# Layer 3's depthwise taps in 64x64 tiles, by a table of slots

## The chip, the cores and the metric

The kernel runs on one core of a Trainium2 chip. The metric is device time in microseconds (us), the median of the timed runs.

## What is computed

Four layers work on x of 4 samples, 256 channels, 48x48 positions, in float32. Layer 0 is an attention over eight heads with normalised queries and keys, layer 1 a gate from depthwise convolutions, layer 2 a second attention; each adds its result to x. Layer 3 is what the change touches:

```
def _L3_conv_ref(x, attn_w1, attn_w2, refine_w, refine_b):
    p = jnp.mean(x, axis=(2, 3))
    h = leaky_relu(p @ attn_w1.T, SLOPE)
    a = sigmoid(h @ attn_w2.T)
    y = x * a[:, :, None, None]
    y = conv_general_dilated(y, refine_w, (1, 1), 'SAME', feature_group_count=C)   # 3x3 depthwise
    y = y + refine_b[None, :, None, None]
    mu = mean(y, (2, 3)); var = mean(square(y - mu), (2, 3))
    return leaky_relu((y - mu) * rsqrt(var + EPS), SLOPE)
...
x = x + _L3_conv_ref(_gn(x), ...)
```

`_gn` normalises groups of eight channels of a sample.

## The kernel before, in words

Channels lie on the 128 partitions, in two halves k; a sample is thus two tiles of 128 x 2304, and layer 3 has eight tiles, cut into six slices of 384 columns (8 rows of 48) each. The engines' instruction streams are written out by hand: each engine runs its own in order.

**Before layer 3.** The last unit of layer 2's attention ends with `total_here`, `fold` and `divide`; `w_stats` (L1062) then takes the last statistics of layer 2's output, from which L1335 to L1348 make the scale sc2 and shift bi2. Layer 1 has taps on TensorE too (L893): diagonal weights in 64x64 tiles, taps of a row half written to both column halves of a bank. Attention (L270, L290) uses 64x64 tiles as well, and alternates between the row halves.

**`Pre`** makes a sample ready. A step is one third of a half sample: four 64x64 matmuls (L1377) give layer 2's output in two banks, ACT normalises it into tmp (L1384), DVE or POOL adds it to X (L1408), DVE takes two `bn_stats` (L1413). `first` (L1388) does the whole of the first sample ahead of the loop, `add` (L1396) the later ones inside it. `chain` (L1417) then turns the statistics into the group norm and the channel gate a, by small matmuls and small DVE instructions; `rsqrt` (L168) is a power on POOL. It ends with ACT filling two padded images `pad` of 50 x 50 (L1476), scaled by rsa and shifted by nba.

**`Conv`** works on one tile. `products` (L1495) puts four of the nine taps on TensorE, each a 128x128 diagonal times a shifted window of the pad, for one slice. `taps` (L1508) does the other five for a pair of slices g, on DVE, in PSUM. `evict` (L1519) moves the pair to z on ACT, with bias and sum; `square` (L1531) sums the squares about a centre; `scales` and `shift` (L1538, L1551) make the instance norm, with rsqrt on POOL (in_ri) and a small product on DVE (in_mr, L1553); `scale` (L1557, ACT) and `leak` (L1561, DVE) finish z; `gain` (L1565, POOL, DVE at the end) adds it to X; `store` writes out.

**The order** is the loop at L1608: over the eight tiles, and in each over six slices, a list of ifs says what goes out in which slice, with the tile before (`prev`) finished during this one and `older` stored. The scores' and values' PSUM tiles (sc two pairs of banks, av one) carry the products; pj has two banks.

**The verdict** (L1580 to L1588) checks that the softmax sums are in bounds, once, before layer 3; it decides at the end whether a general path runs, which does not happen here.

Of the kernel before, what the change touches and what calls it, by code (L numbers as in the profile page):

```python
# [74 lines left out]
def usual_path(  # L75
# [8 lines left out]
    ps_sc = ctx.enter_context(tc.tile_pool(name="ps_sc", bufs=2, space=bass.MemoryType.PSUM))  # L84
    ps_av = ctx.enter_context(tc.tile_pool(name="ps_av", bufs=1, space=bass.MemoryType.PSUM))
    ps_pj = ctx.enter_context(tc.tile_pool(name="ps_pj", bufs=2, space=bass.MemoryType.PSUM))

# [987 lines left out]
    PE_TAPS = (0, 1, 2, 3)  # L1075
    DVE_TAPS = (4, 5, 6, 7, 8)
    diag = {}

    def diagonals():

        for k in range(NK):
            xs = xsp.tile([P, NK, SL + 1], F32, tag="xs", name="diag")
            xs = xs.rearrange("p k s -> p (k s)")[:, : len(PE_TAPS) * P]
            diag[k] = xs.rearrange("p (t j) -> p t j", j=P)
            for n, t in enumerate(PE_TAPS):
                nc.gpsimd.tensor_scalar(
                    diag[k][:, n, :], ident, rfw[:, k, t : t + 1], None, ALU.mult
                )
                yield 1
# [260 lines left out]

    W2 = HW + 2
# [5 lines left out]
    GW = 2 * SL  # L1357

# [5 lines left out]
    class Pre:  # L1364


        def __init__(self, n):
            self.n, self.b = n, SEQ[n]
            self.st = small.tile([P, NK, NSL, 6], F32, tag="gn_st", name="gn_st")
            self.steps = [(k, c) for k in range(NK) for c in range(L2C)]  # L1370
# [17 lines left out]
        def first(self, i, eng):  # L1388

            ps = two_banks(i)  # L1390
            self.product(i, [ps[:, h, :SL] for h in range(2)])
            tmp = wk.tile([P, 2, SL], F32, tag="tmp", name="tmp")
            self.normed(i, tmp, ps[:, :, :SL])
            self.gain(i, tmp, eng)

        def add(self, i):  # L1396
            halves = [pj_tile()[:, :SL] for _ in range(2)]
            self.product(i, halves)
            tmp = wk.tile([P, 2, SL], F32, tag="tmp", name="tmp")
            for h in range(2):  # L1400
                self.normed(i, tmp[:, h, :], halves[h])
            self.gain(i, tmp, nc.gpsimd)
# [7 lines left out]
        def stats(self, i):  # L1410
            k, c = self.steps[i]
            for s in (c, c + L2C):
                nc.vector.bn_stats(  # L1413
                    self.st[:, k, s, :], X[self.b][:, k, s * SL : (s + 1) * SL]
                )

        def chain(self):  # L1417

            mv = small.tile([P, NK, 2], F32, tag="gn_mv", name="gn_mv")
            for k in range(NK):  # L1420
                nc.vector.bn_aggr(mv[:, k, :], self.st[:, k].rearrange("p s f -> p (s f)"))
            yield
            ps = pj_tile()
            nc.tensor.matmul(ps[:, 0:NK], lhsT=gmat, rhs=mv[:, :, 0], start=True, stop=True)
            yield
            gm = small.tile([P, NK], F32, tag="gn_gm", name="gn_gm")
            nc.vector.tensor_copy(gm, ps[:, 0:NK])
            dev = small.tile([P, NK], F32, tag="gn_dev", name="gn_dev")
            nc.vector.tensor_sub(dev, mv[:, :, 0], gm)
            sq = small.tile([P, NK], F32, tag="gn_sq", name="gn_sq")  # L1430
            nc.vector.tensor_mul(sq, dev, dev)
            nc.vector.tensor_add(sq, sq, mv[:, :, 1])
            yield
            ps = pj_tile()
            nc.tensor.matmul(ps[:, 0:NK], lhsT=gmat, rhs=sq, start=True, stop=True)
            yield
            gv = small.tile([P, NK], F32, tag="gn_gv", name="gn_gv")
            nc.vector.tensor_scalar(gv, ps[:, 0:NK], GN_EPS, None, ALU.add)
            rs = small.tile([P, NK], F32, tag="gn_rs", name="gn_rs", bufs=6)
            rsqrt(rs, gv)  # L1440
            yield
            yield

            pm = small.tile([P, NK], F32, tag="pm", name="pm")
            nc.vector.tensor_mul(pm, dev, rs)
            nb = small.tile([P, NK], F32, tag="gn_nb", name="gn_nb", bufs=6)
            nc.vector.scalar_tensor_tensor(nb, gm, -1.0, rs, ALU.mult, ALU.mult)
            yield
            ps = pj_tile()
            for k in range(NK):  # L1450
                nc.tensor.matmul(
                    ps[0:D, 0:1], lhsT=w1[:, k, :], rhs=pm[:, k : k + 1],
                    start=k == 0, stop=k == NK - 1,
                )
            raw = small.tile([D, 1], F32, tag="hraw", name="hraw")
            nc.vector.tensor_copy(raw, ps[0:D, 0:1])
            hl = small.tile([D, 1], F32, tag="hl", name="hl")
            nc.vector.scalar_tensor_tensor(hl, raw, SLOPE, raw, ALU.mult, ALU.max)
            yield
            ps = pj_tile()  # L1460
            for k in range(NK):
                nc.tensor.matmul(
                    ps[:, k : k + 1], lhsT=w2[:, k * P : (k + 1) * P], rhs=hl,
                    start=True, stop=True,
                )

            ga = small.tile([P, NK], F32, tag="ga", name="ga")
            nc.scalar.activation(ga, ps[:, 0:NK], AF.Exp, scale=-1.0)
            nc.vector.tensor_scalar(ga, ga, 1.0, None, ALU.add)
            nc.vector.reciprocal(ga, ga)  # L1470
            rsa = small.tile([P, NK], F32, tag="rsa", name="rsa")
            nc.vector.tensor_mul(rsa, rs, ga)
            nba = small.tile([P, NK], F32, tag="nba", name="nba")
            nc.vector.tensor_mul(nba, nb, ga)
            for k in range(NK):
                nc.scalar.activation(  # L1476
                    pads[(self.n * NK + k) % NPAD][:, 1 : 1 + HW, 1 : 1 + HW],
                    X[self.b][:, k, :].rearrange("p (r c) -> p r c", c=HW), AF.Identity,
                    bias=nba[:, k : k + 1], scale=rsa[:, k : k + 1],
                )  # L1480
                yield

    class Conv:


        def __init__(self, i):
# [3 lines left out]
            self.z = big.tile([P, N], F32, tag="qk"[i // 2 % 2], name="z")  # L1490

            self.st = small.tile([P, 2, NG3], F32, tag="in_st", name="in_st", bufs=3)
            self.ps = {}

        def products(self, s):  # L1495
            g = s // 2
            if s % 2 == 0:
                self.ps[g] = two_banks(self.i * NG3 + g)
            for n, t in enumerate(PE_TAPS):
                dr, dc = divmod(t, 3)  # L1500
                nc.tensor.matmul(  # L1501
                    self.ps[g][:, s % 2, :SL].rearrange("p (r c) -> p r c", c=HW),
                    lhsT=diag[self.k][:, n, :],
                    rhs=self.pad[:, s * RS + dr : (s + 1) * RS + dr, dc : dc + HW],
                    start=n == 0, stop=n == len(PE_TAPS) - 1,
                )

        def taps(self, g):  # L1508
            z = self.ps[g][:, :, :SL].rearrange("p h (r c) -> p h r c", c=HW)
            for t in DVE_TAPS:  # L1510
                dr, dc = divmod(t, 3)
                r0 = 2 * g * RS + dr
                src = self.pad[:, r0 : r0 + 2 * RS, dc : dc + HW]
                nc.vector.scalar_tensor_tensor(  # L1514
                    z, src.rearrange("p (h r) c -> p h r c", h=2),
                    rfw[:, self.k, t : t + 1], z, ALU.mult, ALU.add,
                )

        def evict(self, g):  # L1519
            nc.scalar.activation(  # L1520
                self.z[:, g * GW : (g + 1) * GW].rearrange("p (h s) -> p h s", h=2),
                self.ps[g][:, :, :SL], AF.Identity, bias=vec[:, V_RB, self.k : self.k + 1],
                accum_out=self.st[:, 0, g : g + 1],
# [54 lines left out]


    ok = lp.tile([P, 2, LW], F32, name="ok")  # L1580
    nc.vector.tensor_scalar(ok[:, 0, :], lsum, SUM_HI, None, ALU.is_le)
    nc.vector.tensor_scalar(ok[:, 1, :], lmin, SUM_LO, None, ALU.is_ge)
    okm = lp.tile([P, 1], F32, name="okm")
    nc.vector.tensor_reduce(okm, ok, AX.XY, ALU.min)
    ps = pj_tile()
    nc.tensor.matmul(ps[0:1, 0:1], lhsT=okm, rhs=ones[:, 0:1], start=True, stop=True)
    sound = lp.tile([1, 1], mybir.dt.int32, name="sound")
    nc.vector.tensor_scalar(sound, ps[0:1, 0:1], P - 0.5, None, ALU.is_ge)  # L1588

    pres = {0: Pre(0), 1: Pre(1)}  # L1590
# [933 lines left out]
```

## Time and profile before

| what | us |
|---|---|
| runs, median of 3 | 3661.74 (3661.73 to 3662.2) |
| profiled execution, its own time | 3660.4 |
| its span | 3658.6 |
| first matmul of layer 3's convolution (L1501) | starts at 3431.1 |
| last DVE tap (L1514) ends | 3642.2 |
| PE busy, whole span | 3499.3 (96%) |
| DVE busy, whole span | 2617.0 (72%) |
| mean granted TensorE clock | 0.982 of full speed |

The span is the time from the first to the last instruction of one profiled execution; PE is TensorE, DVE VectorE, ACT ScalarE, POOL GpSimd, SP the engine that issues most transfers. On the page, the rows of digits cut the span in 40 slices and give the busy share in tenths. A group's row has the line, the engine, the operation, output <- inputs, shape and count; after the bar its busy time and mean duration in ns; after the next bar the engine's idle time just before it and what ended it.

### The profile page before, as it was taken

Reading aid. Unit: us, or ns where it says so; the run is one execution under the profiler, and the core shown is the slowest. Engines: PE = TensorE matmul, PEld = TensorE weight load, DVE = VectorE, ACT = ScalarE, POOL = GpSimd, SP = SyncE. Lnnn points to the kernel's source line nnn. Section 1 sums busy time; section 2 is a strip of 40 time slices with the busy share of each in tenths; the row PEclk is TensorE's granted clock in tenths of the full one; section 3 lists DMA queues with packets and bytes.
Section 4 is the critical chain, followed back from the end, with each engine's and each line's share of the span. In section 5 each row is a group of like instructions: output and inputs, shape, how many; then the busy total and the mean of one; then the engine's idle time right before and its main releaser. Section 6 shows DMA issues by size and latency. Waiting matters only on the chain. (4 is left out here: it accounts for less than half of the span.)

```text
span 3658.6 us, 86475 instructions
## 1 busy us (share of the span) xinstructions
PE 3499.3 (96%) x36338; PEld 1778.0 (49%) x36338; DVE 2617.0 (72%) x3227; ACT 2381.9 (65%) x3814; POOL 1389.8 (38%) x881
## 2 busy tenths in 40 slices
PE   8999999999999999999999999999999999999685
PEld 4555555454444445544444444444444445654343
DVE  3555555476989786869896868688967687576687
ACT  4665666666875886668758866687588555555353
POOL 2333333333333333333333333333333366664232
PEclk9999999999999999999999999999999999999797
DMA  2111111111111111311111111111111100000001
GB/s 91 47 25 21 27 22 25 21 25 21 26 21 25 21 26 21 77 21 25 21 25 21 25 21 26 21 26 21 30 13 30 13 6 6 6 8 4 26 39 66
DMA packets 113534, 95.52 MB, mean 26 GB/s; under 512 B 56192, under 2 KB 110064, under 8 KB 111600
## 3 DMA queue, kind: packets, MB, share of 16 engines
q1 hardware_dynamic: 110240, 87.73, 13.1%
q8 instruction: 286, 4.69, 0.5%
q10 hardware_dynamic: 2896, 2.18, 0.2%
q14 instruction: 112, 0.92, 0.1%
HBM read 56.97 MB, written 11.80 MB: 19 GB/s over the span
## 5 line engine op out<-in xcount | busy, mean ns | idle before, releaser
L276 ACT ACTIVATE pt<-sc 128x768 f32<-128x768 f32 x1944 | 1475.3, 811 | 768.2 <-PE sc L270 759.9
L301 POOL TENSOR_TENSOR half<-pt 128x768 f32<-128x768 f32 x477 | 948.7, 1990 | 1607.9 <-ACT pt L276 1512.2
L270 PE MATMUL sc<-q,k 64*64 64x384 f32 x13824 | 1273.3, 483 | 5.1 <-ACT pt L276 5.1
L290 PE MATMUL av<-pt,v 64*64 64x384 f32 x13824 | 1276.4, 484 | 0.0
L316 DVE TENSOR_TENSOR acc<-acc,pt 128x768 f32<-128x768 f32 x792 | 962.1, 1215 | 81.0 <-DVE acc L316 1.9
L270 PEld LDWEIGHTS sc<-q,k 64*64 64x64 f32 x13824 | 521.0, 133 | 607.9 <-issue 537.3
L290 PEld LDWEIGHTS av<-pt,v 64*64 64x64 f32 x13824 | 518.6, 133 | 592.2 <-issue 559.5
L316 DVE TENSOR_TENSOR acc<-acc,half 128x768 f32<-128x768 f32 x459 | 475.1, 1035 | 306.3 <-POOL half L301 305.1
L653 DVE SCALAR_TENSOR_TENSOR x<-pj,bo,x 128x384 f32<-128x384 f32 x192 | 118.3, 616 | 435.3 <-PE pj L648 434.8
L826 ACT ACTIVATE prod<-pd,wt 128x256 f32<-128x256 f32 x486 | 335.9, 761 | 0.2
L566 PE MATMUL pj<-xs,w 128*128 128x384 f32 (+1 forms) x720 | 275.4, 505 | 0.9 <-POOL xs L510 0.9
L371 POOL TENSOR_TENSOR o<-o,rinv 128x384 f32<-128x384 f32 x95 | 119.0, 1253 | 358.0 <-DMA rinv<-rinv 336.1
L566 PEld LDWEIGHTS pj<-xs,w 128*128 128x128 f32 x720 | 124.1, 189 | 128.9 <-issue 35.9
L290 PE MATMUL av<-pt,qv 64*64 64x384 f32 x1728 | 178.0, 503 | 0.0
L648 PE MATMUL pj<-o,wo 128*128 128x384 f32 x384 | 162.0, 506 | 14.8 <-DVE x L653 7.2
L270 PE MATMUL sc<-qv,kd 64*64 64x384 f32 x1728 | 172.3, 491 | 2.4 <-ACT pt L276 2.4
L849 DVE TENSOR_REDUCE prod<-prod 128x256 f32<-128x1280 f32 x114 | 168.4, 1477 | 4.1 <-ACT prod L826 4.1
L310 DVE TENSOR_TENSOR acc<-pt 128x768 f32<-128x768 f32 x99 | 150.6, 1521 | 10.7 <-ACT pt L276 10.7
L597 PEld LDWEIGHTS pj<-w,xs 128*128 128x128 f32 x1080 | 134.5, 191 | 24.1
L597 PE MATMUL pj<-w,xs 128*128 128x128 f32 x1080 | 134.9, 275 | 0.0
L367 POOL TENSOR_TENSOR o<-raw 128x384 f32<-128x384 f32 x95 | 117.6, 1238 | 0.0
L582 ACT ACTIVATE k<-pj,bias 128x384 f32<-128x384 f32 x90 | 52.3, 581 | 95.3 <-PE pj L566 94.8
(234 smaller groups left out, 2672.0 us busy)
## 6 DMA issues: line engine op xcount, KB each, us to landing
xs<-in_x_dram SPq DMA_DIRECT2D x90, 384.0 KB
rinv<-rinv SPq DMA_DIRECT2D x208, 94.5 KB
out_dram<-x SPq DMA_DIRECT2D x6, 1152.0 KB
l<-row SPq DMA_DIRECT2D x416, 1.5 KB
w<-in_wqkv_dram SPq DMA_DIRECT2D x32, 192.0 KB
x<-in_x_dram SPq DMA_DIRECT2D x4, 1152.0 KB
x<-in_x_dram SPq DMA_DIRECT2D x9, 384.0 KB
rinv<-ls SPq DMA_DIRECT2D x208, 1.5 KB
```

Of the source, the lines that this page charges most:

```text
L270: nc.tensor.matmul(ps[c * D : (c + 1) * D, h, :SL], lhsT=u["of"]["k"][r, j0 : j0 + D], rhs=u["of"]["q"][r, u["qc"]], start=True, stop=True,)
L276: nc.scalar.activation(pt, ps[:, :, :SL], AF.Exp, scale=u["scale"])
L290: nc.tensor.matmul(u["av"][h * D : (h + 1) * D, half, :SL], lhsT=value(u, j, h)[r], rhs=pt[r, h, :], start=j == 0, stop=j == JB - 1,)
L301: nc.gpsimd.tensor_add(half, pts[0], pts[1])
L310: nc.vector.tensor_add(u["acc"], ready[0], ready[1])
L316: nc.vector.tensor_add(u["acc"], u["acc"], term)
L371: eng.tensor_mul(o, o, u["rinv"])
L566: nc.tensor.matmul(ps[:, :n], lhsT=at["w"][:, k, t, :], rhs=xs[s][:, k, :n], start=k == 0, stop=k == NK - 1,)
L597: nc.tensor.matmul(ps[:, i * P : (i + 1) * P], lhsT=xs[s][:, k, i * P : (i + 1) * P], rhs=at["w"][:, k, 2, :], start=k == 0, stop=k == NK - 1,
L648: nc.tensor.matmul(ps[:, :SL], lhsT=wo[:, p, k * P : (k + 1) * P], rhs=o["o"], start=True, stop=True,)
L826: nc.scalar.activation(bufs[n % 3][:, :, min(n, 1) + i].rearrange("p (r c) -> p r c", c=AS), pd[:, PAD + dr : PAD + dr + AS, PAD + dc : PA ...
L849: nc.vector.tensor_reduce(to, bufs[n % 3][:, :, : min(n, 1) + len(taps)], AX.X, ALU.add)
```

## The change

Eight of the nine taps go to TensorE, in 64x64 tiles; DVE keeps the middle one (4). A slice uses two banks, each a PSUM tile of its own in a pool of six. Bank h holds the products of channel half h: even taps in its own half of the partitions, odd taps in the other. DVE adds the middle tap to the first sum and writes z; ACT copies the second sum with the bias to `part`, across to the channels' own partitions; a `join` of the pair adds both and sums them.

```
-    PE_TAPS = (0, 1, 2, 3)
-    DVE_TAPS = (4, 5, 6, 7, 8)
+    PE_TAPS, DVE_TAP = (0, 1, 2, 3, 5, 6, 7, 8), 4
...
-                    diag[k][:, n, :], ident, rfw[:, k, t : t + 1], None, ALU.mult
+                    diag[k][:, n, :], ident2, rfw[:, k, t : t + 1], None, ALU.mult
...
+    rb_x = lp.tile([P, NK], F32, name="rb_x")
+    for to, fr in zip(HALVES, HALVES[::-1]):
+        nc.sync.dma_start(rb_x[to, :], vecs[fr, V_RB, :])
...
         def products(self, s):
...
+            self.ps[s] = [ps_one.tile([P, 512], F32, tag="one", name="one") for _ in HALVES]
+            now["ps"] = self.ps[s][0]
+            last = len(PE_TAPS) // 2 - 1
+            for n in range(last + 1):
+                for h, r in enumerate(HALVES):
+                    for e in range(2):
+                        nc.tensor.matmul(
+                            self.ps[s][h][HALVES[h ^ e], :SL].rearrange(
+                                "p (r c) -> p r c", c=HW
+                            ),
+                            lhsT=diag[self.k][r, 2 * n + e, :],
+                            rhs=self.window(r, s, PE_TAPS[2 * n + e]),
+                            start=n == 0, stop=n == last,
+                        )
...
         def evict(self, s):
...
+            for h, r in enumerate(HALVES):
                 nc.vector.scalar_tensor_tensor(
+                    z[r], self.window(r, s, DVE_TAP), rfw[r, self.k, DVE_TAP : DVE_TAP + 1],
+                    self.ps[s][h][r, :SL].rearrange("p (r c) -> p r c", c=HW),
+                    ALU.mult, ALU.add,
+                )
+                nc.scalar.activation(
+                    self.part[g][HALVES[1 - h], s % 2, :], self.ps[s][1 - h][r, :SL],
+                    AF.Identity, bias=rb_x[r, self.k : self.k + 1],
+                )
+
+        def join(self, g):
+            z = self.z[:, g * GW : (g + 1) * GW]
+            nc.vector.tensor_tensor_reduce(
+                z, z, self.part[g].rearrange("p h s -> p (h s)"), 1.0, 0.0, ALU.add, ALU.add,
+                self.st[:, 0, g : g + 1],
+            )
```

The loop is replaced by a table: each job is put at a slot t (one slot per slice, 48 and a few more) with a rank, and the slots are written out one after the other.

```
+    FRONT, PRODUCT, CONV, EVICT, SMALL, NEXT, THEN, LAST, OUT = range(9)
...
+    def put_step(t, n, i, gap=1):
+        at(t, PRODUCT, lambda: pres[n].multiply(i))
+        at(t, NEXT, lambda: pres[n].evict(i))
+        at(t, OUT, lambda: pres[n].gain(i, pres[n].tmp, nc.gpsimd))
+        at(t + gap, LAST, lambda: pres[n].stats(i))
...
+    for n in range(1, B):
+        t = (n - 1) * SAMPLE
+        if n > 1:
+            for i in range(STEPS):
+                put_step(max(3, t - 10 + 2 * i), n, i)
+        put_chain(t + 4, pres[n].chain())
+        for k in range(NK):
+            for i in range(NG3):
+                at(t + 10 + k * NSL + 2 * i, LAST, lambda n=n, k=k, i=i: pres[n].pad(k, i))
...
+    def put_tile(t, cv, final):
         for s in range(NSL):
+            at(t + s, CONV, lambda s=s: cv.products(s))
+            at(t + s + 1, EVICT, lambda s=s: cv.evict(s))
+        for g in range(NG3):
+            at(t + 2 * g + 3, NEXT, lambda g=g: cv.join(g))
+            at(t + 2 * g + 4, THEN, lambda g=g: cv.square(g))
+        at(t + 3, THEN, cv.centre)
+        dt = 9 if final else 10
+        at(t + dt, THEN, cv.scales)
+        at(t + dt + 1, FRONT, cv.shift)
+        for g, cols in enumerate(THIRDS):
+            t0, dt = (t + 10 + g, 1) if final else (t + 11 + 2 * g, 2)
+            at(t0, THEN, lambda cols=cols: cv.scale(cols))
+            at(t0 + 1, NEXT, lambda cols=cols: cv.leak(cols))
+            eng = nc.vector if final else nc.gpsimd
+            at(t0 + 1 + dt, OUT, lambda cols=cols: cv.gain(cols, eng))
+            at(t0 + 1 + dt, OUT, lambda cols=cols: cv.store(cols))
```

Further: pad, scale, leak, gain and store now go in thirds of a tile. The chain's small products land in columns 384 and up of a slice's first bank, and its parts have a slot each. Three steps of the second sample (`filled`) are multiplied during the first sample's chain, in the sc and av banks, before these are given back for the pool of six. The verdict moves into slots 6 and 7 of the table. In the built program's order the first three products of layer 3 stand ahead of the last `w_stats` on TensorE. Lines of the changed kernel that the prediction names: products L1541, DVE's tap L1559, ACT's copy L1564, join L1571, square L1583, shift L1603, scale L1609, leak L1613, gain L1617.

## The prediction

> **What bounds the kernel now.** I read the page first, then busy time by stretch for the last 370 us, then the groups and the timeline of that stretch.
>
> ```profile
> PE   8999999999999999999999999999999999999685
> DVE  3555555476989786869896868688967687576687
> PEclk9999999999999999999999999999999999999797
> ```
>
> TensorE (PE) bounds the first 3395 us; there the two programs differ only in the small GpSimd (POOL) instructions that build the diagonals. Layer 3 is the last two or three slices, so at most some 7% of the time can move.
>
> ```profile
> 3436.00:3458.00 22.00, 17.91 (x76) 8.17 (x72) 15.08 (x21) 7.93 (x15) 7.39 (x5) 1.00 0.00 1
> 3458.00:3480.00 22.00, 19.84 (x61) 10.22 (x62) 15.26 (x34) 9.55 (x16) 6.65 (x5) 0.77 0.00 1
> 3600.00:3620.00 20.00, 17.34 (x53) 9.35 (x51) 19.08 (x21) 6.20 (x10) 5.87 (x4) 1.00 0.14 59
> ```
>
> Columns: stretch, length, busy time of PE, weight loads, DVE, ACT, POOL, then the clock. In layer 3 DVE is the fullest (19.08 of 20 late on); ACT has less than half. The clock holds 1.00 with PE 81% busy and falls after a PE gap of 3.4 us that ends at 3458.4. The groups say what fills DVE:
>
> ```profile
> L1514 DVE SCALAR_TENSOR_TENSOR sc<-pad,rfw,sc 128x768 f32<-128x768 f32 x80 | 81.7, 1021 | 2.3
> L1514 DVE SCALAR_TENSOR_TENSOR av<-pad,rfw,av 128x768 f32<-128x768 f32 x40 | 40.6, 1016 | 1.1
> L1520 ACT ACTIVATE z<-sc,vec 128x768 f32<-128x768 f32 x16 | 14.4, 900 | 57.2 <-DVE sc L1514 50.9 <-PEq L2450 6.3
> ```
>
> Five taps make 5.25 us for two slices, 126 us in all, and ACT's eviction waits 51 us for them. From nba (3428.6) to the last tap (3642.2) are 213.6 us for 24 pairs of slices, 8.9 a pair; then 16.4 us to the end.
>
> **TensorE, part by part.** Before, a slice is 4 matmuls of 128x128x384, 8 instructions, 2.6 us. After, it is 16 of 64x64, 32 instructions. Attention runs 16 such instructions in 1.29 us, so 2.58. [...] Attention alternates row groups; the new loop issues two tiles of one group in a row. If they took turns, two tiles would run instead of four: 5.2 us a slice. But layer 1's taps (L893) have exactly this order:
>
> ```profile
> 3046.18 2.87 PE L893 MATMUL pj<-pd,diag 64*64 64x256 f32 x48
> 3048.82 1.52 PE L290 MATMUL av<-pt,qv 64*64 64x384 f32 x16
> ```
>
> 48 in 2.64 us are 55 ns each; times 384/256 and 32, 2.64 us. I take that: eight taps cost what four did. With a step (0.65) and small products a pair is 5.5 to 6.1 us on PE, not the bound.
>
> **DVE and ACT, per pair of slices.** Removed: 5.25 of taps on DVE, 1.1 of eviction on ACT. Added: DVE, four taps of 64x384 from PSUM. No row has 64 partitions; 128x384 from PSUM (L653) is 0.617, and ACT's 64x384 (0.576) is near its 128x384 (0.581), so 0.617. ACT, four `part` copies at 0.576 (L1014, which also crosses partitions). And the join, a sum with a running total, no row: SBUF add 0.96 (DVE L1567) plus a read of the total near ACT's 0.19, 1.12 together. [...] Leak (L1563), that kind with two fp32 SBUF sources but without a total, does 128x768 in 0.95[...]; I take 1.12 and keep 1.92 for the range; below nothing is excluded, since it is new work. Thirds in place of whole tiles: pad 0.9 for 768 columns (2.31 whole), scale 0.95, leak 0.96.
>
> **A wait that comes in.** In the changed program's order of instructions DVE's second tap of a slice waits for ACT's first copy, and ACT's second copy for DVE's first tap, since they read the same bank. So DVE and ACT meet in every slice, 1.24 us for the meeting, and a slice costs that plus the longer of what either does between: what is queued behind the second tap (join, leak, sums) stands still. PE waits for both before it can take the banks again, three slices on. Even slots with a step: ACT 1.22 (normalise, L1384 pair) + 1.06 square + 0.89 pad = 3.17; DVE only the leak. Odd: DVE join + 1.02 for two sums = 2.1, ACT 0.95. The work alternates, so the longer sides add up.
>
> **POOL's hold.** A DVE instruction with two SBUF inputs waits for a running POOL add:
>
> ```profile
> 3527.06 1.83 POOL L1567 TENSOR_TENSOR x<-x,z 128x768 f32<-128x768 f32 x1
> 3527.32 1.58 DVE L1553 SCALAR_TENSOR_TENSOR in_mr<-in_mv,in_ri 128x1 f32<-128x1 f32 x1
> ```
>
> One element took 1.58 us and ended with POOL's. Taps, with one side in PSUM, stay at 1.02. Join, leak and shift can be held. In a step pair POOL adds from 1.5 to 5.1 us (two of 1.81), and the join comes at 4.4: held 0.6.
>
> **The sum in pairs** (even slot, meeting, odd slot, meeting).
> - Step: 3.17 + 1.24 + (0.6 + 1.12 + 1.02 + 0.05) + 1.24 = 8.4. Every third has the scales: in_ri comes at 2.8, POOL starts the next add before shift, which is held to 4.6; join to 7.5, sums, meeting: 9.85.
> - No step: 1.95 (square, pad) + 1.24 + 1.15 + 1.24 = 5.6; with scales, shift held to 4.5, join to 7.3: 8.55.
> - Slots 1 to 12 (no leaks at first, steps in 0 to 4): from nba pads and the three filled slices keep DVE to 8.8, then meetings end at 10.0, 13.3, 16.6, 21.1, 25.5, 30.5, 34.0, 38.2, 41.7, 46.3, 51.2, 54.6. Each is the longer side: at slot 2, ACT's normalise and pad, 2.1.
> - Slots 13 to 26: 5 x 8.4 + 2 x 9.85 + 1.3 (statistics chain) = 63. Slots 27 to 48: 7 x 5.6 + 4 x 8.55 + 1.4 = 74.8. Together 192.4, against 213.6.
>
> **Start.** The order puts the first three products ahead of the last w_stats, and the verdict (L1581 to L1588) moves into the loop. ACT then starts when bi2 is there, 3408.5 for 3411.1: -2.6. Two products between the statistics' matmuls on a cold PE (16 instructions at half clock, 2.6 us, over a cover of 1.3) put +1.3 back. A shorter w_stats may save up to 2 more, nothing may too; I take 0.3: nba at 3427.0. The verdict costs DVE 1.3 in slots 6 and 7, counted. Diagonals: 16 POOL instructions of 128x64 for 8 of 128x128 (0.6 to 1.4 each), between adds with 2 to 10 us of POOL idle behind them: 0; were the cover gone, about 0.4 x 16 = 6 at most, 0 taken. rb_x, two small loads on SP behind x_back, is due 30 us later: 0. Stores are 24 of a third for 9, on SP, which nobody waits for but the end: 0.
>
> **Tail.** After the last tap DVE has leak and join, then a leak before the scales; in_ri is followed on POOL by an add that holds shift 1.8: 20.3 us instead of 16.4.
>
> End: 3427.0 + 192.4 + 20.3 = 3639.7, 18.9 below the profiled span of 3658.6; its own time was 3660.4, the median 3661.7, so about 3642.
>
> **Rivals.**
> - *Engines slide past each other*: waits average out and DVE's sum counts. Taps 56, joins 27, leaks 23, sums 18, scales 12, chains 8, rest 7 = 151, holds 11, tail waits and store 13: 3427 + 175 = 3602, with the 3.1 us between span and median 3605. For: three slices of banks; against: both waits per slice.
> - *The join runs at half rate*: 0.8 x 24 = 19, mostly on the DVE side of odd slots: 3661. [...]
> - *Slower: tiles of one row group take turns.* A slice costs 5.2, a pair 11.35 with its step and small products, 10.7 without: 13 x 11.35 + 11 x 10.7 = 265, 52 over now, with the longer tail and the earlier start 54: 3716. It decides from 8.9 a pair, so from some 4 us a slice. [...]
>
> **How the numbers follow.** Meeting and hold as above 0.55 (own range 3628 to 3654), sliding 0.22 (3595 to 3625), half-rate join 0.17 (3652 to 3668), turns 0.06. A measurement tells 0.2% (7.3 us) from no change: faster below 3654.4, so 0.53 + 0.22 + 0.04 = 0.79; same 0.02 + 0.08 = 0.10; slower 0.05 + 0.06 = 0.11. The range 3608 to 3664 leaves out half of sliding, the top of the half-rate join, and turns.
>
> **What would show it.** L1541: 32 instructions every 2.6 us when unblocked, clock 1.0. L1559 about 0.6 each, DVE idle before its second tap on ACT's copy, ACT idle before its second copy on DVE's tap. L1571 near 0.96[...]. L1603 and L1571 ending with a POOL add. Tiles of 27 us with steps, 20 without. Wrong if DVE is over 92% busy throughout (sliding), or PE is.

## The result and the profile after

| | before | changed |
|---|---|---|
| runs, median | 3661.73 (3658.35 to 3662.2) | 3637.64 (3636.78 to 3639.25) |
| ratio to before | 1 | 0.9937, interval 0.9919 to 0.9954 |
| span of the profiled execution | 3658.6 | 3637.4 |

24.1 us less by the medians, 0.63% by the ratio; the forecast was 3642 in a range of 3608 to 3664. The three rows of the changed kernel's page that answer to those shown of before:

```profile
PE   8999999999999999999999999999999998999786
...
DVE  3555555577889787778797877777977778575678
...
PEclk9999999999999999999999999999999999999798
```

The DVE rows differ in the middle too, where both programs do the same work; only the last three slices tell of the change. Busy time by stretch in layer 3 of the changed kernel (columns as in the prediction's table: length, PE, weight loads, DVE, ACT, POOL, clock):

```profile
3436.00:3458.00 22.00, 22.00 (x240) 10.37 (x236) 17.01 (x35) 15.29 (x25) 9.11 (x5) 0.88 0.01 2
3458.00:3480.00 22.00, 20.95 (x250) 9.62 (x246) 16.55 (x44) 13.76 (x26) 6.68 (x5) 1.00 0.01 1
3580.00:3600.00 20.00, 17.05 (x204) 7.44 (x200) 16.53 (x29) 16.43 (x26) 6.40 (x5) 1.00 0.16 61
```

Late in the layer DVE had been at 19.08 of 20. Now DVE and ACT each are busy for 16.5 of 20 and PE for 17: no engine is full, so waits between them set the time. (Early, PE reads 22.00 of 22; half_taps below shows that it is not what the slots wait for there either.) The groups name the waits:

```profile
L1541 PE MATMUL one<-pad,diag 64*64 64x384 f32 x1536 | 136.6, 501 | 19.0 <-ACT pad L1511 11.8 <-issue 5.1 <-ACT part L1564 1.8
...
L1559 DVE SCALAR_TENSOR_TENSOR z<-pad,rfw,one 64x384 f32<-64x384 f32 x96 | 58.8, 612 | 26.3 <-ACT part L1564 14.7 <-ACT ga L1491 5.5 <-PE one L1541 3.7
L1564 ACT ACTIVATE part<-one,rb_x 64x384 f32<-64x384 f32 x96 | 55.3, 576 | 45.7 <-DVE z L1559 38.2 <-issue 4.5 <-PE one L1541 1.0
...
L1613 DVE SCALAR_TENSOR_TENSOR z<-z 128x768 f32<-128x768 f32 x24 | 27.0, 1130 | 0.9 <-ACT z L1609 0.2
L1571 DVE CUSTOM_DVE_ANT_0 z<-z,part 128x768 f32<-128x768 f32 x24 | 26.0, 1084 | 0.5
...
L1603 DVE SCALAR_TENSOR_TENSOR in_mr<-in_mv,in_ri 128x1 f32<-128x1 f32 x8 | 12.4, 1556 | 4.4 <-POOL in_ri L170 4.4
```

ACT's copies wait 38.2 us for DVE's taps, DVE's taps 14.7 us for ACT's copies; both hardly wait for PE (3.7 and 1.0). The only tile that the two rows share is `one`. The one-element shift (L1603) takes 1556 ns on average. Both are in one pair of slices of a late tile, on DVE and POOL (start, duration, group):

```profile
3588.75 0.96 DVE L1613 SCALAR_TENSOR_TENSOR z<-z 128x768 f32<-128x768 f32 x1
...
3590.41 0.21 DVE L1596 TENSOR_SCALAR in_ve<-in_ve,in_mv 128x1 f32<-128x1 f32 x1
...
3590.79 0.55 POOL L170 TENSOR_TENSOR in_ri<-in_ve,mhalf 128x1 f32<-128x1 f32 x1 [10.30 <-ACT pad L1511]
3591.31 3.58 POOL L1617 TENSOR_TENSOR x<-x,z 128x768 f32<-128x768 f32 x2
3591.38 1.76 DVE L1603 SCALAR_TENSOR_TENSOR in_mr<-in_mv,in_ri 128x1 f32<-128x1 f32 x1 [0.75 <-POOL in_ri L170]
3593.17 1.26 DVE L1559 SCALAR_TENSOR_TENSOR z<-pad,rfw,one 64x384 f32<-64x384 f32 x2
3593.81 0.58 ACT L1564 ACTIVATE part<-one,rb_x 64x384 f32<-64x384 f32 x1 [2.51 <-DVE z L1559]
...
3594.46 1.24 DVE L1571 CUSTOM_DVE_ANT_0 z<-z,part 128x768 f32<-128x768 f32 x1
```

After the scales DVE waits 0.75 us for in_ri, then its shift lasts 1.76 us, to 3593.14, half-way through POOL's two adds of 3.58 (0.16 where these adds are left out, in no_pool_gain below), and only then come the taps; ACT's second copy has waited 2.51 us for them.

**Layer 3 by itself.** The last reciprocal of the softmax sums (L381 before, L382 after) marks the end of what both kernels do alike. It starts at 3394.97 in the profiled execution of before and at 3397.73 in that of the changed kernel; over all profiled executions of this study it lies between 3394.7 and 3400.7. A difference of a few us between two kernels is therefore read from that mark on, one profiled execution of each. "Start" runs from the mark to the first fill of a pad (nba), "loop" from there to the end of the last DVE tap, "tail" to the end of the span:

| kernel | start | loop | tail | sum | median of the runs | ratio to before (interval) |
|---|---|---|---|---|---|---|
| before | 33.7 | 213.6 | 16.4 | 263.6 | 3661.73 | 1 |
| forecast | 32.0 | 192.4 | 20.3 | 244.7 | 3642 | |
| changed | 31.7 | 186.9 | 21.1 | 239.7 | 3637.64 | 0.9937 (0.9919 to 0.9954) |
| rows_alternate | 32.4 | 186.2 | 21.1 | 239.7 | 3635.06 | 0.9926 (0.9910 to 0.9943) |
| half_taps | 31.7 | 184.0 | 21.1 | 236.7 | 3637.64 | 0.9935 (0.9919 to 0.9952) |
| verdict_first | 35.3 | 186.5 | 21.1 | 242.9 | 3638.80 | 0.9936 (0.9919 to 0.9952) |
| shift_behind | 31.7 | 180.7 | 21.1 | 233.5 | 3628.26 | 0.9908 (0.9892 to 0.9925) |
| shift_gain | 32.4 | 179.8 | 21.1 | 233.3 | 3629.89 | 0.9914 (0.9897 to 0.9930) |
| no_pool_gain | 32.4 | 175.9 | 16.8 | 225.1 | 3621.31 | 0.9892 (0.9874 to 0.9910) |
| copies_later | 32.4 | 174.8 | 21.6 | 228.8 | 3622.85 | 0.9893 (0.9877 to 0.9910) |
| shift_copies | 31.7 | 170.2 | 21.8 | 223.7 | 3622.27 | 0.9891 (0.9875 to 0.9908) |
| holds_copies | 31.8 | 167.6 | 22.6 | 222.0 | 3619.92 | 0.9881 (0.9865 to 0.9898) |

Each ratio is to executions of before from the same session. Medians of neighbouring rows are not told apart by their intervals. Where the start is 32.4 the first normalise itself came 0.7 later, and slot 1 of the loop ended 0.5 to 0.6 sooner, as the first slice took 4.8 us for 5.4 in the changed kernel. I read this as the clock coming back to 1.00 before the slice was over: its last four weight loads (3441.05 in rows_alternate) stand 0.45 us ahead of the next four, where the changed kernel has 0.64 at clock 0.50 and 0.32 at 1.00. The sum is untouched, as rows_alternate shows; so two rows of different start are compared by the sum.

### The profile page after: what moved, and what is told of

It is laid out like the page before. It is cut to its first block, busy times and chain, and to the rows that moved or that the text cites. A ratio compares the mean times of both kernels' runs of the same rounds, so it can differ in the third digit from the quotient of the medians.

```text
span 3637.4 us, 88927 instructions
## 1 busy us (share of the span) xinstructions
PE 3488.9 (96%) x37490; PEld 1762.7 (48%) x37490; DVE 2600.2 (71%) x3268; ACT 2423.3 (67%) x3889; POOL 1387.0 (38%) x886
## 3 DMA queue, kind: packets, MB, share of 16 engines
q8 instruction: 296, 4.85, 0.5%
## 5 line engine op out<-in xcount | busy, mean ns | idle before, releaser
L1541 PE MATMUL one<-pad,diag 64*64 64x384 f32 x1536 | 136.6, 501 | 19.0 <-ACT pad L1511 11.8
L598 PEld LDWEIGHTS pj<-w,xs 128*128 128x128 f32 x1080 | 134.5, 191 | 24.1
```

The source lines that it names most:

```text
L598: nc.tensor.matmul(ps[:, i * P : (i + 1) * P], lhsT=xs[s][:, k, i * P : (i + 1) * P], rhs=at["w"][:, k, 2, :], start=k == 0, stop=k == NK - 1,
L1541: nc.tensor.matmul(self.ps[s][h][HALVES[h ^ e], :SL].rearrange("p (r c) -> p r c", c=HW), lhsT=diag[self.k][r, 2 * n + e, :], rhs=self.win ...
```

## The experiments

All are edits of the changed kernel.

**The order of the row halves on TensorE** (rows_alternate)

```
-                for h, r in enumerate(HALVES):
-                    for e in range(2):
+                for e in range(2):
+                    for h, r in enumerate(HALVES):
```

> The matmuls of a slice in another order: row half by row half in turn, as attention does it, where the changed kernel issues two tiles of one row half in a row. If two tiles of one half in a row cost overlap[...], the alternating order is faster: less than the 0.322 us per four instructions that the changed kernel's trace shows at full clock, and the cold first slice under 5.4 us. If the order does not matter: 0.322 again, the loop within 0.5 us of 186.9, and the time within 2 us of the changed kernel's.

Weight loads of the changed kernel, two tiles of one row half in a row, at full clock:

```profile
3448.25 0.16 PEld L1541 LDWEIGHTS one<-pad,diag 64*64 64x64 f32 x4 [0.17 <-issue]
3448.57 0.16 PEld L1541 LDWEIGHTS one<-pad,diag 64*64 64x64 f32 x4 [0.17 <-issue]
```

and with the halves in turn:

```profile
3443.43 0.16 PEld L1541 LDWEIGHTS one<-pad,diag 64*64 64x64 f32 x4 [0.17 <-issue]
3443.76 0.16 PEld L1541 LDWEIGHTS one<-pad,diag 64*64 64x64 f32 x4 [0.16 <-issue]
...
3444.40 0.16 PEld L1541 LDWEIGHTS one<-pad,diag 64*64 64x64 f32 x4 [0.16 <-issue]
```

Four instructions every 0.32 us in both (3443.43 to 3444.40 is three such steps), and the same 239.7 in all. The first slice took less, as the expectation had it for an order that matters:

```profile
3437.19 4.82 PE L1541 MATMUL one<-pad,diag 64*64 64x384 f32 x32 [4.07 <-issue]
```

But it took 4.83 to 4.85 in shift_gain, no_pool_gain and copies_later as well, where the order is the old one: this goes with the start of 32.4, not with the order. On these 64x64 tiles the halves in turn are no faster than two tiles of one half in a row.

**Half of the taps left out** (half_taps): `last = 1` for `last = len(PE_TAPS) // 2 - 1`.

> Only four of the eight taps on TensorE are issued (16 instructions a slice for 32; the output lacks four taps). If TensorE is not the bound (DVE and ACT meeting): the cold first slice ends 2.7 us earlier, of which some is caught up later anyway, else nothing: -1 to -3 us. If TensorE with its 2.6 to 3.5 us a slice still sets slots 1 to 9 (3.4 us a slot): -8 us there; if it also sets pairs with steps, -12 or more.

The output lacks four taps. The loop is 2.9 shorter. The changed kernel's clock (0.50) in the stretch ahead of its first slice, and that slice:

```profile
3404.00:3441.00 37.00, 19.95 (x112) 8.32 (x116) 20.68 (x50) 12.75 (x16) 9.89 (x22) 0.50 0.13 55
```

```profile
3435.36 5.40 PE L1541 MATMUL one<-pad,diag 64*64 64x384 f32 x32 [4.07 <-issue]
```

A late stretch of half_taps, which answers to the last row of the changed kernel's table above:

```profile
3580.00:3600.00 20.00, 11.33 (x108) 3.74 (x100) 16.70 (x30) 16.44 (x26) 5.90 (x4) 0.89 0.15 60
```

Its first slice takes 2.84. Slot 1 ends 10.1 us after nba instead of 12.7, and that lead is still there at slot 12 (51.0 for 53.9) and at the end (184.0 for 186.9); from slot 13 on each pair of slices lasts as long as before the edit, within 0.1 us, though PE is busy for 11.33 of 20 and not 17. So TensorE is not what the pairs wait for, but the cold first slice costs its full price (5.40 for 2.84, and 2.9 in the loop): I had expected part of it to be caught up.

**The verdict back in front** (verdict_first): the chain `judge()` runs ahead of the first products again, not from slot 6.

> The verdict is put back ahead of layer 3's first products; then these also stand behind the last statistics on TensorE, as in the kernel before. Theory: first normalise 2.6 to 3.3 us later and nba 2 us later counted from the last reciprocal of the softmax sums, the loop up to 0.5 shorter: +1.5 us (0.5 to 2.5). Rival (the start is set by the statistics chain, which both orders share): within 0.5 us.

The first normalise comes 3.4 later after the mark (16.28 for 12.85), nba 3.6 later, the loop is 0.4 shorter: 3.2 in all, more than expected. Beyond before's 33.7 it is 1.6, because two steps' products (`multiply`, 16 instructions) still stand between the chain's small matmuls:

```profile
3424.90 2.84 PE L1382 MATMUL sc<-y,Ww 64*64 64x384 f32 x16
...
3425.98 0.16 DVE L1462 TENSOR_TENSOR pm<-gn_dev,gn_rs 128x2 f32<-128x2 f32 x1 [0.81 <-POOL gn_rs L170]
...
3427.66 0.58 PE L1469 MATMUL pj<-pm,w 128*64 128x1 f32 x4
```

pm is there at 3426.1 and its matmul starts at 3427.7. The medians (3638.80 and 3637.64) do not resolve this.

**The shift behind the taps** (shift_behind): `at(t + dt + 1, SMALL, cv.shift)` for `FRONT`. In a slot, FRONT stands ahead of everything and SMALL just behind DVE's taps.

> The shift goes behind the two taps of its slot. If what it costs is the way over POOL (0.75 us of waiting for in_ri), the taps hide it: -0.75 x 8 = -6 us, and -2 x 8 = -16 if the 1.76 us of the shift itself are that latency too. If it is POOL's hold, the shift is held until the first of two adds ends (1.9 + 0.75 + 1.8 after the leak starts), and the join behind it meets the second add instead of the taps: 0 to -3 us.

**and the adds of z a slot earlier** (shift_gain): also `(t + 11 + 2 * g, 1)` for `(t + 11 + 2 * g, 2)`.

> As the last, and POOL's adds of z stand one slot earlier, so that the second third's is ahead of in_ri on POOL and only one add follows in_ri. Hold theory: leak 0.95, scales 0.95, taps 1.3, shift until 4.5, join 1.0, taps 1.3: a pair of 6.7 for 8.3, -1.6 x 7 = -11 us (-6 to -13). Rival, latency alone: as the last run, no further gain.

shift_behind takes 6.2 from the loop, 5.8 of it in the four pairs with scales and no step: 8.3 (7.9 in one) became 6.7. Its rows, DVE and then POOL:

```profile
3588.22 1.30 DVE L1559 SCALAR_TENSOR_TENSOR z<-pad,rfw,one 64x384 f32<-64x384 f32 x2
3589.55 1.16 DVE L1603 SCALAR_TENSOR_TENSOR in_mr<-in_mv,in_ri 128x1 f32<-128x1 f32 x1
3590.63 0.95 DVE L1571 CUSTOM_DVE_ANT_0 z<-z,part 128x768 f32<-128x768 f32 x1
```

```profile
3588.36 0.55 POOL L170 TENSOR_TENSOR in_ri<-in_ve,mhalf 128x1 f32<-128x1 f32 x1 [10.22 <-ACT pad L1511]
3588.87 4.38 POOL L1617 TENSOR_TENSOR x<-x,z 128x768 f32<-128x768 f32 x2
```

The taps hide the wait for in_ri, the shift is held for what is left of the first add. I had expected the join to be held next; it was not (0.95), and POOL's two adds lasted 4.38 instead of 3.58, 0.80 more. By these durations POOL was held here, and DVE went first. So the adds a slot earlier had nothing left to save, and shift_gain has the same sum. In the two pairs with a step and scales (9.2) nothing is won, as a step's add follows in_ri on POOL: in one it is a chain's sum of 128x2 that is held, 1.80 us in both kernels (not because the shift had moved away, as I took it to be below), in the other the shift is held by the second add instead of the first, 1.78 for 1.76.

**POOL's adds of z left out** (no_pool_gain): `gain` is only called for the last tile.

> POOL's adds of z to X are left out for seven of the eight tiles (the output of these lacks layer 3; the last tile keeps its three adds). Hold theory: shift 0.15 for 1.76 and join 0.96 for 1.25 in four pairs with scales and no step (-1.9 each), joins 0.4 in five pairs with steps, leak and shift in the tail some 4: about -14 us (-9 to -17). Rival (DVE's long instructions end with POOL's by chance, or other work covers them): within 2 us.

Seven of the eight tiles are not added to X here. 11.0 less in the loop, 4.3 in the tail, 14.6 in all. Its groups:

```profile
L1571 DVE CUSTOM_DVE_ANT_0 z<-z,part 128x768 f32<-128x768 f32 x24 | 23.0, 957 | 0.6
L1613 DVE SCALAR_TENSOR_TENSOR z<-z 128x768 f32<-128x768 f32 x24 | 22.9, 958 | 0.9 <-ACT z L1609 0.2
L1603 DVE SCALAR_TENSOR_TENSOR in_mr<-in_mv,in_ri 128x1 f32<-128x1 f32 x8 | 4.5, 558 | 4.4 <-POOL in_ri L170 4.4
```

Join, leak and shift lose 3.0, 4.1 and 7.9 of busy time on DVE: 15.0 together, and the layer lost 14.6. So nearly all of what DVE's instructions lose to these adds lies on the path.

**ACT's copies a slot later** (copies_later): the copies leave `evict` and become a job of their own.

```
             at(t + s + 1, EVICT, lambda s=s: cv.evict(s))
+            at(t + s + 2, EVICT, lambda s=s: cv.copy(s))
```

> ACT's two copies of a slice stand one slot later than DVE's taps, so that no tap waits for a copy (DVE waits once a pair, in the join). Meeting theory: in pairs with a step (7.5 to 8.2 us now) the longer sides no longer add up, ACT's own sum of about 6.7 or DVE's of 5.6 with a hold is left: some 0.8 us in 5 pairs and 0.5 in 2 with scales, so about -5 us (-3 to -7). Pairs with scales and no step (8.27) are DVE's own chain: 0. Pairs without either (5.5) are ACT's sum: 0. Rival (the waits are cover for something else, PE or POOL): within 1 us of the changed kernel.

12.1 less in the loop; 0.7 of that is the start's, and the tail gives 0.5 back, so 10.9 in the layer, twice what I had expected. Slots 1 to 12 end at 50.9 for 53.9, pairs with a step last 6.5 to 8.7 for 7.5 to 8.7, and, against the expectation, late pairs with neither step nor scales 4.8 to 5.0 for 5.5 to 5.6. I had taken ACT's 5.5 as the floor of such a pair; it is one only on average. Over a tile of three pairs (19.4 before this edit, 18.0 with it) ACT needs 16.5 and draws on the 8.3 of the pair with scales, once no tap waits for a copy any more. Its DVE by group:

```profile
L1553 DVE SCALAR_TENSOR_TENSOR z<-pad,rfw,one 64x384 f32<-64x384 f32 x96 | 58.8, 612 | 7.3 <-PE one L1541 3.0 <-ACT ga L1491 1.8
L1571 DVE CUSTOM_DVE_ANT_0 z<-z,part 128x768 f32<-128x768 f32 x24 | 27.6, 1150 | 0.9 <-ACT part L1564 0.2
```

Waits for ACT's copies are gone from the taps (L1553 here), and the join waits 0.2 us for them in all.

**Both** (shift_copies, then holds_copies, in which the third leak of a tile also goes behind the next join and the adds of z a slot earlier)

> The shift behind the two taps of its slot, and ACT's copies one slot later. In the run with the late copies DVE was busy but for the 0.75 us of in_ri in each tile (18.0 us a tile without steps), so DVE's own sum set it. If so, the two add up: that 0.75 and about 1 us of the held shift go, until ACT's sum of 3 x 5.5 = 16.5 us a tile is reached: 16.5 to 17 a tile, -1.2 x 8 = -8 to -10 us beside the late copies alone, -18 to -22 beside the changed kernel. If the two remove the same waiting instead, no more than the late copies alone (-12 in the loop).

> As the last, and POOL's adds of z a slot earlier, and the third leak of a tile behind the join of the next slot, so that no add of z is queued directly behind in_ri. If the holds still cost something there: tiles without steps at ACT's 16.5, DVE with 1 us to spare; -2 to -5 us beside the last run. If ACT already sets the tile, or the holds only move to other instructions (as a chain's 0.57 us add took 1.80 where the shift had moved away): within 1.5 us of the last run.

shift_copies is 4.6 below the late copies alone in the loop (5.1 in the layer), half of what was expected of it; beside the changed kernel the layer is 16.0 shorter, where the two edits by themselves gave 10.9 and 6.2, so they nearly add up. Late pairs now last 5.6 to 6.6, a tile 17.7 and not the 16.5 to 17 that I had expected: the shift is still held there, 1.2 us. In holds_copies no add of z stands directly behind in_ri but in the last tile, and in the tiles without steps the shift takes 0.16. The loop is at 167.6, 2.6 less, with 0.8 given back in the tail: 1.7 in the layer, a little under what was expected. It has the shortest layer of all, 17.7 us less than the changed kernel, and the lowest median, 3619.92, though the intervals do not tell it from the rows just above. A late stretch of it:

```profile
3570.00:3590.00 20.00, 20.00 (x248) 12.69 (x244) 18.87 (x34) 19.44 (x30) 7.82 (x5) 1.00 0.16 63
```

PE, DVE and ACT are all at 94% or more here: a tile lasts 16.4 us, in which ACT's instructions stand back to back (15.97 us busy), and little waiting is left to take away.

## Why the prediction was right, point by point

It named the mechanism and the time within 4.4 us. Over the layer it was 5.0 too slow (244.7 for 239.7); in the forecast's terms: start -0.3, slot 1 +2.7, slots 2 to 12 -3.4, 13 to 26 -3.8, 27 to 48 -1.0, tail +0.8. So 8.5 too much and 3.5 too little partly cancel: that the total came this close is in part luck, the mechanism is not.

- **TensorE: right, but for the cold slice.** 32 instructions at 8 x 0.322 = 2.58 us at clock 1.00; L893 was the row to trust, and the order of the row halves makes no difference (0.32 us per four instructions and 239.7 in all with either). The step that failed is slot 1 ending at 10.0: the clock read 0.50 from about 3404 to 3441, and the first slice took 5.4 us. I had halved the clock for the two products of the start and forgotten it for this slice. With the slice at 2.84 (half_taps) slot 1 ends at 10.1, as forecast, and the 2.7 us stay to the end.
- **DVE and ACT: right.** The tap is 0.612 for 0.617, the copy 0.576. The join was mis-sized: 0.96 when not held, with a read of 0.08 largely under it, where the forecast had 1.12; that is some 0.15 each, 3.6 us at most over 24 joins. The half rate (1.92, an estimate of mine that no trace showed) did not occur: the mean is 0.957 without POOL's adds of z (no_pool_gain).
- **The meeting: right.** There were 40 waits of over 0.15 us of one of the two engines for the other in 48 slices, and taking the wait out shortened the layer by 10.9. The pairs came near their sums: 5.5 to 5.6 for 5.6 late in the loop (up to 6.5 where a statistics chain runs); 8.2 to 8.3 for 8.55 (7.9 in one); 7.5 to 8.7, 8.2 on average, for 8.4; 9.2 for 9.85. Of the 3.8 in slots 13 to 26, pairs with a step are 1.2, with scales 1.3, and the 1.3 set apart for the chain did not come on top. The 3.4 of slots 2 to 12 is not worked out.
- **POOL's hold: right**, 14.6 us by no_pool_gain. What the forecast had not got is that POOL's adds can last longer as well, 4.38 for 3.58 in shift_behind.
- **Start: right**, 2.0 less for the forecast 1.6. The order ahead of the statistics is worth 3.2 us, and the products between the chain's matmuls take some 1.6 back.
- **Tail: the sum right, by luck, the split not**, 21.1 for 20.3. Of the 4.7 over before's 16.4, no_pool_gain takes back 4.3: nearly all is hold, on the shift (1.75 for 0.16) and on three leaks (2.37 for 0.96, and two in 3.34 for 1.88). The forecast had 1.8 of hold, at the shift alone, and put the rest down to DVE's added leak and join.
- **Rivals.** The engines sliding past each other is not what this kernel does; with the late copies it is nearer to it, and that is worth 11 us and not the 37 of the forecast (3642 less 3605), since the first twelve slots still take 50.9 and the holds stay where they are. That rival's sum was also 3 us short: 96 taps at 0.617 are 59, not 56. Tiles of one row group taking turns, 5.2 us a slice, did not occur: 2.58 at clock 1.00. The 5.2, twice 2.58, was an estimate of mine that no trace showed.

What is not settled is why the part ahead of layer 3 varies by some 6 us between executions. It was not tried, and it is as large as several effects above.

## What to carry to other kernels

When two engines read two buffers crosswise and each waits for the other, a slice costs the meeting plus the longer of their other work, and long sides that alternate add up; a slot of distance between the two reads (the copies a slot later) brings that nearer to the larger of the two sums: 10.9 us of the layer here. A tiny instruction behind a round trip to another engine (the shift: 0.75 us of waiting for in_ri, then 1.76) belongs behind work that does not need it, which was worth 6.2 us here, and an add of two SBUF tiles on POOL should not be queued just where DVE has such an instruction to do: late in the layer the shift took 1.2 us with such an add behind in_ri (shift_copies) and 0.16 without (holds_copies). When TensorE has been idle now and then ahead of a stage (busy for 19.95 of 37 us here), read its clock there (0.50), price the first piece of the stage at it (5.40 us), and do not count on catching up (2.9 us stayed to the end).

## What was not expected of the hardware

- Two adds on POOL lasted 3.58 us where DVE's shift took 1.76 beside them (changed) and 4.38 where the shift took 1.16 and a join its 0.95 (shift_behind). That POOL was held for the join is read from these durations; it was not isolated.
- The held instructions can be tiny: one of 128x1 (L1603) took 1.76 us and one of 128x2 (L1451) 1.80 in the changed kernel, for 0.15 and 0.16 at other places of it.
- The first slice's 32 matmul instructions took 5.40 us at clock 0.50, the next slice's 2.77 at 1.00; with half of the taps the first slice took 2.84 at 0.50. The clock had been at 0.50 for 37 us, in which PE was busy for 20.
